# Message-passing layer on one core: the dst table in float32, picked by half blocks on half of the partitions each

## The chip, the cores and the metric

The kernel runs on one NeuronCore of a Trainium2 chip. The metric is the device time of one execution in microseconds (us). Engines are named as the profile names them: PE (TensorE; PEld are its weight loads), DVE (VectorE), ACT (ScalarE), POOL (GpSimd), SP (SyncE, which here only issues DMAs). "SPq" and "ACTq" are DMA issues of these two queues.

## The reference, cut to what matters

```python
h = relu(layernorm(x))                                   # x: 12500 nodes x 64
e = silu(concat(h[src], h[dst], dist) @ eW1 + eb1)       # 212500 edges, eW1: 129 x 128
e = silu(e @ eW2 + eb2)                                  # 128 -> 128
agg = segment_sum(e, src, 12500)
out = x + silu(concat(h, agg) @ nW1 + nb1) @ nW2 + nb2
```

The edges come sorted by dst. All is float32.

## The kernel before, in words

The first product is taken apart: `h[src] @ eW1[:64]` and `h[dst] @ eW1[64:128]` are computed once for each node and kept in two DRAM tables, `ta` (with the bias `eb1` in it) and `tb`. Each entry is held as three bfloat16 numbers (high, middle and low part of the float32 value), 384 numbers in a row. Node n has the place l = n // 100 in the bucket b = n mod 100, so there are 100 buckets of 125 nodes. The work has four stages.

1. **Prologue** (pools `pro`, `norm`, `nab`, `nps`). x is loaded and normalised in five pieces of 20 buckets. `product(1, ...)` makes `tb` for four buckets at a time: matmuls, a copy of the high part (L183), then the rest and the two lower parts (L187 to L190), then a DMA (L192). From src and dst it makes the rows that the blocks compare with (`rows`), for each block the lowest dst of its window (`base_i`), and from the edge weights their three bfloat16 parts (`aux`, `parts3` on DVE and ACT).
2. **Sends.** The edges go in 208 blocks of 1024. `load(s + 2, 1)` issues on SP, for block s, the compare rows three blocks ahead (`bc`, L378) and the window of 112 rows of `tb` and the weight rows of `pick` two blocks ahead (`win` L384, `pick` L386). The start of the window is a register value that SP loads from `base_i` (L383). `count(s + 1)` makes on DVE the one-hot matrix `pick` of dst within the window (L395), the one-hot matrix of the src bucket (`oh`, L397), its running count (`run`, L400) and the count at each edge's own bucket (L408). `send(s)` reads the rank of each edge (L427), multiplies `pick` by `win` (`qp`, L435: for 128 edges three matmuls, one for each bfloat16 part, over 112 node rows and three rows more, which hold the edge weights' parts in `pick` and the weight's row of eW1 in `win`), copies the result to `qs` (ACT, L442), sets the target rows `to` (DVE, L445) and scatters each 128 edges with one indirect DMA from POOL to the DRAM table `q` of the chunk (L454), in which each bucket has a piece of its own. `to` has 4 buffers and `qs` 8, so four blocks of either.
3. **Steps.** The blocks form 11 chunks: the first of 8 blocks, with one tile of 128 rows for each bucket, the others of 20 blocks, with two tiles. When all of a chunk's rows are in DRAM they are read back in 25 batches of four buckets (`fetch`: `qt` from `q`, L499, and `a3` from `ta`, L504, both on SP, five batches ahead). A step takes four tiles of 128 edges: the place within the bucket is spread over the partitions and made one-hot (`s_lr` L521, `s_one_t` L526), the row of `ta` is added while the tile is transposed (`s_pt` L535, L542), then silu, eW2, silu (`s_p2` L573), and the segment sum by one more one-hot matrix (`s_one` L553, `s_seg` L587, `s_add` L598).
4. **Nodes.** With the last chunk's batches the node network runs (`nodes`, L325 to L353).

The order on PE, DVE, ACT and SP is the program's own (`manual_schedule`): `turn` lists the parts of a step with four places between them, at which pieces of the sends of the next chunk are put in, spread evenly (`marks`), three pieces for a block. `sources` (the `ta` table) is fed in at the same places, during the first two chunks. In the prologue a scheduler orders the engines.

PSUM: pool `mm` (4 buffers) serves `lr`, `pt`, `qp`, `ab`, `z` and `o` in turn, `p2` has two, `misc` and `seg` one each.

Of the kernel before, what the change touches and what calls it, by code (L numbers as in the profile page):

```python
# [28 lines left out]
F32 = mybir.dt.float32  # L29
F16 = mybir.dt.float16  # L30
BF16 = mybir.dt.bfloat16
I32 = mybir.dt.int32
# [6 lines left out]
P = 128  # L39
L = 125  # L40
WL = 112
BLK = 1024
TB = BLK // P
# [14 lines left out]
def tile_gnn(ctx: ExitStack, tc: tile.TileContext, x, src, dst, ew, eW1, eb1, eW2, eb2, nW1, nb1, nW2, nb2, out):  # L58
# [39 lines left out]
    def rows16(dma, to, of):  # L98

        for part in (slice(0, WL), slice(WL, L)):  # L100
            dma(to[part], of[part])
# [10 lines left out]
    eb1r = const.tile([1, 2, H], F32, name="eb1r")  # L112
    for t in range(2):
        nc.gpsimd.dma_start(eb1r[:, t, :], rows_of(eb1, 1))
# [31 lines left out]
    nc.vector.tensor_copy(nodes1, nodes_i)  # L146
    ones = const.tile([1, P], F32, name="ones")
# [15 lines left out]
    tb = dram.tile([P * NB, 3 * H], BF16, name="tb")  # L163
    rows = dram.tile([NP, 2, 2, BLK], BF16, name="rows")
    aux = dram.tile([NP, 2, 3, BLK], BF16, name="aux")
# [3 lines left out]
    def product(s, b0, hr, ps, tag, sb, sb2, queue):  # L169

        parts = sb2.tile([P, G, 3, H], BF16, name="parts")
        by = parts.rearrange("l (i a) s h -> l a i s h", a=2)
        rest = sb.tile([P, 2, G // 2, H], F32, name="prest", tag="e1")
        abs_ = []
        for a in range(2):

            half = slice(a * D, (a + 1) * D)
            ab = ps.tile([P, G // 2, H], F32, name="ab", tag=tag)
            if s == 0:
                nc.tensor.matmul(ab, ones, eb1r, start=True, stop=False)  # L180
            for i in range(G // 2):
                nc.tensor.matmul(ab[:, i], hr[half, i, :], w1[half, s, :], start=s == 1, stop=s == 1 or i == G // 2 - 1)
            nc.scalar.copy(by[:, a, :, 0, :], ab)  # L183
            abs_.append(ab)
        yield
        for a in range(2):
            nc.vector.tensor_tensor(rest[:, a], abs_[a], by[:, a, :, 0, :], op=OP.subtract)  # L187
# [9 lines left out]
    base_i = const.tile([1, 2, NP], I32, name="base_i")  # L197
    NW = 4
    wins = [const.tile([P, 3, H], BF16, name=f"win{i}") for i in range(NW)]

    with tc.tile_pool(name="pro", bufs=1) as pro, tc.tile_pool(name="norm", bufs=2) as np_, tc.tile_pool(
# [12 lines left out]
        ewR = pro.tile([NP, PAIR], F32, name="ewR")  # L214
        pad_i = pro.tile([1, PAD], I32, name="pad_i")
        nc.gpsimd.memset(pad_i, N)
        pad_f = pro.tile([1, PAD], F32, name="pad_f", tag="pad_i")
        nc.gpsimd.memset(pad_f, 0.0)
        vec = lambda v, lo, n, m: bass.AP(tensor=v.tensor, offset=v.offset + lo, ap=[[m, n], [1, m]])
        for to, v, pad in (  # L220
            (dstR, dst, vec(dst, E - PAD, 1, PAD)),
            (srcR, src, pad_i),
            (ewR, ew, pad_f),
# [41 lines left out]
        fv = f.rearrange("p (g e) -> p g e", g=2)  # L265
        lo = pro.tile([NP, 2], F32, name="lo")
        nc.vector.tensor_reduce(lo, fv, AX.X, OP.min)
        nc.vector.tensor_scalar(lo, lo, float(N - WL), None, op0=OP.min)
        hi = pro.tile([NP, 2], F32, name="hi")
        nc.vector.tensor_reduce(hi, fv, AX.X, OP.max)  # L270
        lot = nps.tile([1, 2, NP], F32, name="lot", tag="tr")
        for g in range(2):
# [5 lines left out]
        nc.vector.tensor_tensor(  # L278
            rowsS[:, :, 0, :], fv, lo[:, :, None].to_broadcast([NP, 2, BLK]), op=OP.subtract
        )  # L280
# [15 lines left out]
        auxS = pro.tile([NP, 2, 3, BLK], BF16, name="auxS")  # L296
        ev = ewR.rearrange("p (g e) -> p g e", g=2)
        parts3(pro, auxS[:, :, 0, :], auxS[:, :, 1, :], auxS[:, :, 2, :], ev, [NP, 2, BLK], tag="t")
        nc.sync.dma_start(aux, auxS)


# [12 lines left out]


        d3 = pro.tile([P, 3, H], BF16, name="d3")
        parts3(pro, d3[:, 0, :], d3[:, 1, :], d3[:, 2, :], w1d, [P, H])
        for win in wins:
            nc.sync.dma_start(win[WL : WL + 3, :, :], d3[:3, :, :])

# [36 lines left out]
    with tc.tile_pool(name="ld", bufs=4) as ld, tc.tile_pool(name="ld2", bufs=NQ) as ld2, tc.tile_pool(  # L357
# [14 lines left out]
        def load(s, ahead=0):  # L372

            if s + ahead < nblocks:
                p, g = (s + ahead) // 2, (s + ahead) % 2
                bc = ld.tile([P, 2, BLK], BF16, name="bc")
                r = rows[p, g]
                nc.sync.dma_start(bc[:WL], bass.AP(tensor=r.tensor, offset=r.offset, ap=[[0, WL], [1, 2 * BLK]]))  # L378
                blk[s + ahead] = [bc]
            if 0 <= s < nblocks:  # L380
                p, g = s // 2, s % 2
                win = wins[s % NW]
                at = nc.sync.value_load(base_i[:, g, p : p + 1], min_val=0, max_val=N - WL)  # L383
                nc.sync.dma_start(win[:WL].rearrange("p s f -> p (s f)"), tb[bass.ds(at, WL), :])  # L384
                pick = ld.tile([P, BLK], BF16, name="pick")
                nc.sync.dma_start(pick[WL : WL + 3, :], aux[p, g])  # L386
                blk[s] += [win, pick]

        def count(s):
# [4 lines left out]
            bc, win, pick = blk[s]  # L394
            nc.vector.tensor_scalar(pick[:WL, :], bc[:WL, 0, :], part[:WL, :], None, op0=OP.is_equal)  # L395
            oh = wk.tile([NB, BLK], F16, name="oh")
            nc.vector.tensor_scalar(oh, bc[:NB, 1, :], part[:NB, :], None, op0=OP.is_equal)  # L397
            yield
            run = wk.tile([NB, BLK], F16, name="run")
# [17 lines left out]
        def send(s):  # L417
# [4 lines left out]
            _, win, pick, run = blk.pop(s)  # L422
# [5 lines left out]
            yield  # L428
            for t0 in range(0, nt, G):
                qs = qsp.tile([P, G, W], F32, name="qs")  # L430
                qp = mm.tile([P, G, H], F32, name="qp", tag="mm")
                m = min(G, nt - t0)
                for t in range(m):
                    for i in range(3):
                        nc.tensor.matmul(  # L435
                            qp[:, t, :],
                            pick[: WL + 3, (t0 + t) * P : (t0 + t + 1) * P],
                            win[: WL + 3, i, :],
                            start=i == 0,
                            stop=i == 2,  # L440
                        )
                nc.scalar.copy(qs[:, :m, :H], qp[:, :m, :])  # L442
# [380 lines left out]
```

## Time and profile before

| | |
|---|---|
| median of 3 runs | 3321.53 us (3317.69 to 3334.8) |
| the profiled execution | 2708.9 us, its span 2706.9 us |
| mean granted TensorE clock in the profile | 0.915 |
| busy: PE, PEld, DVE, ACT, POOL | 2321.1, 2168.2, 1846.2, 1204.1, 1723.0 us |
| indirect DMAs of POOL (L454) | 1661 of 1030 ns |
| `qp` matmuls (L435) | 4983 of 227 ns |
| DMA | 612.85 MB, mean 226 GB/s |

The duration of a matmul is that of one passing through a pipeline, so matmuls that follow each other overlap: what one costs is read from where the next group starts in the timeline. The profiled execution is shorter than the runs by 612.6 us; all durations and places in time below are the profiled one's.

### The profile page before, as it was taken

Reading aid. Unit: us, or ns where it says so; the run is one execution under the profiler, and the core shown is the slowest. Engines: PE = TensorE matmul, PEld = TensorE weight load, DVE = VectorE, ACT = ScalarE, POOL = GpSimd, SP = SyncE. Lnnn points to the kernel's source line nnn. Section 1 sums busy time; section 2 is a strip of 40 time slices with the busy share of each in tenths; the row PEclk is TensorE's granted clock in tenths of the full one; section 3 lists DMA queues with packets and bytes.
Section 4 is the critical chain, followed back from the end, with each engine's and each line's share of the span. In section 5 each row is a group of like instructions: output and inputs, shape, how many; then the busy total and the mean of one; then the engine's idle time right before and its main releaser. Section 6 shows DMA issues by size and latency. Waiting matters only on the chain. (4 is left out here: it accounts for less than half of the span.)

```text
span 2706.9 us, 61144 instructions
## 1 busy us (share of the span) xinstructions
PE 2321.1 (86%) x23583; PEld 2168.2 (80%) x23583; DVE 1846.2 (68%) x3287; ACT 1204.1 (44%) x2247; POOL 1723.0 (64%) x1691
## 2 busy tenths in 40 slices
PE   1656688799799699799979979979979979979998
PEld 0445577799699699799879979979979979978886
DVE  5745468688588588678768768868858868743332
ACT  2522234355355355355445435535535545534442
POOL 1036577777777777777777777777777777750000
PEclk9755689899899899999989989989989989989998
DMA  6477867987787697697797787788688758644441
GB/s 180 170 210 208 246 226 227 284 276 231 237 280 244 211 288 247 200 312 245 214 293 254 224 274 252 246 247 269 229 248 272 244 185 267 216 173 127 137 128 33
DMA packets 388692, 612.85 MB, mean 226 GB/s; under 512 B 47232, under 2 KB 294401, under 8 KB 387877
## 3 DMA queue, kind: packets, MB, share of 16 engines
q1 hardware_dynamic: 269560, 423.47, 48.7%
q0 software_dynamic: 53760, 122.94, 13.3%
q10 hardware_dynamic: 65074, 62.46, 9.4%
q8 instruction: 188, 3.08, 0.5%
q14 instruction: 110, 0.90, 0.1%
HBM read 393.49 MB, written 215.18 MB: 225 GB/s over the span
## 5 line engine op out<-in xcount | busy, mean ns | idle before, releaser
L454 POOL DMA_INDIRECT q<-qs,to x1661 | 1710.3, 1030 | 679.2 <-issue 386.4
L546 ACT ACTIVATE e<-pt 128x512 f32<-128x512 f32 x525 | 313.7, 597 | 926.5 <-PE pt L542 765.1
L573 PE MATMUL p<-w,e 128*128 128x128 f32 x4200 | 578.7, 282 | 102.3 <-ACT p L567 102.3
L573 PEld LDWEIGHTS p<-w,e 128*128 128x128 f32 x4200 | 523.6, 196 | 117.1 <-ACT p L567 104.3
L526 DVE TENSOR_SCALAR oneT<-lr,part 125x512 bf16<-125x512 f32 x525 | 392.3, 747 | 325.8 <-PE lr L521 325.7
L587 PE MATMUL seg<-one,e 128*128 128x125 f32 x4200 | 581.2, 282 | 19.8 <-DVE aggT L598 14.6
L587 PEld LDWEIGHTS seg<-one,e 128*128 128x128 f32 x4200 | 523.6, 196 | 22.6 <-ACT qs L442 11.7
L400 DVE TENSOR_TENSOR_SCAN run<-oh,end,misc 100x1024 f16<-100x1024 f16 x197 | 461.1, 2340 | 6.4 <-PE misc L427 5.8
L542 PE MATMUL pt<-oneT,a 125*128 125x256 bf16 (+1 forms) x3300 | 440.1, 272 | 0.0
L435 PE MATMUL qp<-win,pick 115*128 115x128 bf16 x4983 | 369.1, 227 | 37.1 <-DVE oneT L526 30.4
L442 ACT COPY qs<-qp 128x512 f32<-128x512 f32 x416 | 243.3, 585 | 286.5 <-PE qp L435 218.3
L435 PEld LDWEIGHTS <-pick 115*128 115x128 bf16 x4983 | 330.4, 102 | 45.3 <-issue 40.8
L553 DVE TENSOR_TENSOR one<-nodes,qt 128x500 f32<-128x500 f32 x525 | 352.2, 671 | 0.7 <-PE seg L587 0.5
L542 PEld LDWEIGHTS <-a 125*128 125x128 bf16 x3300 | 317.8, 99 | 33.5
L535 PE MATMUL pt<-ident,qt 128*128 128x128 f32 x2100 | 329.5, 281 | 3.1 <-DVE prest L187 2.2
L577 ACT ACTIVATE e<-p 128x512 f32<-128x512 f32 x525 | 313.2, 597 | 12.9 <-PE p L573 9.6
L567 ACT COPY p<-b2f 128x512 f32<-128x512 f32 x525 | 311.8, 594 | 0.0
L598 DVE TENSOR_TENSOR aggT<-aggT,seg 128x500 f32<-128x500 f32 x250 | 168.2, 673 | 152.5 <-PE seg L587 152.3
L521 PE MATMUL lr<-identb,qt 128*125 128x128 bf16 x2100 | 210.6, 224 | 62.2 <-DMA qt<-q 62.2
L521 PEld LDWEIGHTS <-qt 128*125 128x125 bf16 x2100 | 187.2, 140 | 64.0 <-DMA qt<-q 63.3
L535 PEld LDWEIGHTS pt<-ident,qt 128*128 128x128 f32 x2100 | 227.6, 144 | 4.0 <-DVE prest L187 2.3
L408 DVE TENSOR_TENSOR run<-run,oh 100x1024 f16<-100x1024 f16 x208 | 144.3, 694 | 7.1
(118 smaller groups left out, 1264.4 us busy)
## 6 DMA issues: line engine op xcount, KB each, us to landing
qt<-q SPq DMA_DIRECT2D x250, 576.0 KB
a<-ta SPq DMA_DIRECT2D x275, 384.0 KB
bc<-rows SPq DMA_DIRECT2D x208, 448.0 KB
q<-zeros ACTq DMA_DIRECT2D x40, 1462.5 KB
q<-qs,to POOLq DMA_INDIRECT x1661
win<-tb SPq DMA_DIRECT2D x208, 84.0 KB
tb<-parts SPq DMA_DIRECT2D x25, 384.0 KB
ta<-parts SPq DMA_DIRECT2D x25, 384.0 KB
```

The lines of the kernel that those rows point to most:

```text
L400: nc.vector.tensor_tensor_scan(run, oh, nil.to_broadcast([NB, BLK]), carry.get(c, 0.0), op0=OP.add, op1=OP.add)
L435: nc.tensor.matmul(qp[:, t, :], pick[: WL + 3, (t0 + t) * P : (t0 + t + 1) * P], win[: WL + 3, i, :], start=i == 0, stop=i == 2,)
L454: i = nc.gpsimd.indirect_dma_start(out=q[:], out_offset=bass.IndirectOffsetOnAxis(ap=to[:k, t : t + 1], axis=0), in_=qs[:k, t - t0, :], in ...
L521: nc.tensor.matmul(lr[:L, t, :], loc[:, at : at + 1].to_broadcast([P, L]), identb, start=True, stop=True)
L526: nc.vector.tensor_scalar(oneT, st[k].pop("lr")[:L], part1[:L, :], None, op0=OP.is_equal)
L535: nc.tensor.matmul(pt[:, t, :], qt[:, j, :H], ident, is_transpose=True, start=t == 0, stop=False, skip_group_check=True)
L542: nc.tensor.matmul(pt[:, cols, :], a3[:L, b, i, :], oneT[:, cols, :], start=False, stop=i == 2, skip_group_check=True)
L546: nc.scalar.activation(e1, pt, AF.Silu)
L553: nc.vector.tensor_tensor(one, nodes1[:, None, :].to_broadcast([P, G, L]), qt[:, j : j + G, H : H + 1].to_broadcast([P, G, L]), op=OP.is_e ...
L573: nc.tensor.matmul(p2[:, t, :], e1[:, t, :], w2, start=False, stop=t == G - 1, skip_group_check=True)
L577: nc.scalar.activation(e2, p2, AF.Silu)
L587: nc.tensor.matmul(item[2][:, b, :], e2[:, t, :], one[:, t, :], start=j % n == 0, stop=j % n == n - 1)
```

## The change

`tb` holds plain float32 rows of 128 (512 bytes where there were 768). `product(1, ...)` therefore only copies its PSUM tiles and sends them off. The window of a block is taken apart in two: each half of a block (512 edges) has a window of 48 nodes (`WL`) of its own, the first on partitions 0 to 49, the second on 64 to 113 (`HB = 64`). `pick` is float32 of 128 x 512: one instruction on DVE makes both halves (`same` is the partition's number within its half, `plus` is 1 on a row of ones). Behind the 48 rows stand the edge weight's row, now loaded in float32 straight from the input, and the row of ones, against which `win` holds the weight's row of eW1 and the bias `eb1`. So the bias leaves `product(0, ...)`, and `aux` and its three parts are gone. A tile of 128 edges takes one float32 matmul over 50 rows where there were three bfloat16 ones over 115; the matmuls of the two halves alternate, and all eight of a block stand in one piece of the program (the `qs` copies too), where there were four tiles in each of two pieces.

On SP a block has two DMAs for `bc`, one for `bb` (the bucket rows), two for `win`, each with a register load before it, and two for the weights, where there were three DMAs and one register load. The weights' DMAs (`weights`) follow the DVE instruction that writes `pick`, since they overwrite a row of it.

```diff
-WL = 112
+WL = 48
+HB = 64
+HALF = BLK // 2
...
+    nc.vector.tensor_scalar(plus, part, HB - 0.5, None, op0=OP.is_gt)
+    nc.vector.scalar_tensor_tensor(same, plus, -float(HB), part, op0=OP.mult, op1=OP.add)
+    nc.vector.tensor_scalar(plus, same, float(WL + 1), None, op0=OP.is_equal)
+    nc.vector.scalar_tensor_tensor(same, plus, -1e6, same, op0=OP.mult, op1=OP.add)
...
-    tb = dram.tile([P * NB, 3 * H], BF16, name="tb")
+    tb = dram.tile([P * NB, H], F32, name="tb")
-    aux = dram.tile([NP, 2, 3, BLK], BF16, name="aux")
...
     def product(s, b0, hr, ps, tag, sb, sb2, queue):
...
-            if s == 0:
-                nc.tensor.matmul(ab, ones, eb1r, start=True, stop=False)
...
+        if s:
+            got = sb2.tile([P, G, H], F32, name="got")
+            for a in range(2):
+                nc.scalar.copy(got.rearrange("l (i a) h -> l a i h", a=2)[:, a], abs_[a])
+            yield
+            queue.dma_start(tables[s][:, b0 : b0 + G, :], got)
+            return
...
-    wins = [const.tile([P, 3, H], BF16, name=f"win{i}") for i in range(NW)]
+    wins = [const.tile([P, H], F32, name=f"win{i}") for i in range(NW)]
+    for win in wins:
+        nc.vector.memset(win, 0.0)
+        for a in range(2):
+            for i, row in enumerate((w1d, eb1b)):
+                at = a * HB + WL + i
+                nc.gpsimd.dma_start(win[at : at + 1, :], row[:1, :])
...
-        auxS = pro.tile([NP, 2, 3, BLK], BF16, name="auxS")
-        ev = ewR.rearrange("p (g e) -> p g e", g=2)
-        parts3(pro, auxS[:, :, 0, :], auxS[:, :, 1, :], auxS[:, :, 2, :], ev, [NP, 2, BLK], tag="t")
-        nc.sync.dma_start(aux, auxS)
...
         def load(s, ahead=0):
...
-                bc = ld.tile([P, 2, BLK], BF16, name="bc")
-                nc.sync.dma_start(bc[:WL], bass.AP(tensor=r.tensor, offset=r.offset, ap=[[0, WL], [1, 2 * BLK]]))
+                bc = ld.tile([P, HALF], BF16, name="bc")
+                for a in range(2):
+                    of = bass.AP(tensor=r.tensor, offset=r.offset + a * HALF, ap=[[0, HB], [1, HALF]])
+                    nc.sync.dma_start(bc[a * HB : (a + 1) * HB, :], of)
+                bb = ld.tile([P, BLK], BF16, name="bb")
+                nc.sync.dma_start(bb[:112], bass.AP(tensor=r.tensor, offset=r.offset + BLK, ap=[[0, 112], [1, BLK]]))
...
-                at = nc.sync.value_load(base_i[:, g, p : p + 1], min_val=0, max_val=N - WL)
-                nc.sync.dma_start(win[:WL].rearrange("p s f -> p (s f)"), tb[bass.ds(at, WL), :])
-                pick = ld.tile([P, BLK], BF16, name="pick")
-                nc.sync.dma_start(pick[WL : WL + 3, :], aux[p, g])
+                for a in range(2):
+                    h = 2 * g + a
+                    at = nc.sync.value_load(base_i[:, h, p : p + 1], min_val=0, max_val=N - WL)
+                    nc.sync.dma_start(win[a * HB : a * HB + WL, :], tb[bass.ds(at, WL), :])
+                pick = ld.tile([P, HALF], F32, name="pick")
+        def weights(s):
+            if s < nblocks:
+                pick = blk[s][3]
+                for a in range(2):
+                    e0 = s * BLK + a * HALF
+                    m = min(HALF, E - e0)
+                    if m > 0:
+                        of = bass.AP(tensor=ew.tensor, offset=ew.offset + e0, ap=[[m, 1], [1, m]])
+                        nc.sync.dma_start(pick[a * HB + WL : a * HB + WL + 1, :m], of)
         def count(s):
...
-            nc.vector.tensor_scalar(pick[:WL, :], bc[:WL, 0, :], part[:WL, :], None, op0=OP.is_equal)
+            nc.vector.tensor_scalar(pick, bc, same, plus, op0=OP.is_equal, op1=OP.add)
...
             yield
+            weights(s)
             run = wk.tile([NB, BLK], F16, name="run")
...
         def send(s):
...
+            qps = [mm.tile([P, G, H], F32, name="qp", tag="mm") for _ in range(2)]
+            for t in range(G):
+                for a in range(2):
+                    half = slice(a * HB, a * HB + WL + 2)
+                    if a * G + t < nt:
+                        nc.tensor.matmul(
+                            qps[a][:, t, :], pick[half, t * P : (t + 1) * P], win[half, :], start=True, stop=True
+                        )
+            halves = []
             for t0 in range(0, nt, G):
-                for t in range(m):
-                    for i in range(3):
-                        nc.tensor.matmul(
-                            qp[:, t, :],
-                            pick[: WL + 3, (t0 + t) * P : (t0 + t + 1) * P],
-                            win[: WL + 3, i, :],
-                            start=i == 0,
-                            stop=i == 2,
-                        )
-                nc.scalar.copy(qs[:, :m, :H], qp[:, :m, :])
+                nc.scalar.copy(qs[:, :m, :H], qps[t0 // G][:, :m, :])
```

## The prediction

> **What bounds the kernel now.** I read the page first: its span, the busy times and the costliest group.
>
> ```profile
> span 2706.9 us, 61144 instructions
> ...
> PE 2321.1 (86%) x23583; PEld 2168.2 (80%) x23583; DVE 1846.2 (68%) x3287; ACT 1204.1 (44%) x2247; POOL 1723.0 (64%) x1691
> ...
> L454 POOL DMA_INDIRECT q<-qs,to x1661 | 1710.3, 1030 | 679.2 <-issue 386.4
> ```
>
> PE looks like the bound. But a POOL that is busy 64% of the span may be full while it has work, so I asked what POOL waited for (total us, times, longest us):
>
> ```profile
> POOL q L454 <- issue: 386.4, 1267, 0.4
> POOL q L454 <- ACT qs L442: 154.8, 18, 143.2
> POOL q L454 <- DMA q<-qs,to: 36.5, 110, 1.7
> ```
>
> The 143.2 us is the time ahead of the first scatter. The rest is almost all a fixed 0.30 us ahead of each one. The timeline of POOL gives the ends and the rhythm:
>
> ```profile
> 172.13 1.17 POOL L454 DMA_INDIRECT q<-qs,to  x1 [143.24 <-ACT qs L442]
> ...
> 1356.63 0.97 POOL L454 DMA_INDIRECT q<-qs,to  x1 [0.30 <-issue]
> 1357.91 0.96 POOL L454 DMA_INDIRECT q<-qs,to  x1 [0.30 <-issue]
> ...
> 2417.58 0.88 POOL L454 DMA_INDIRECT q<-qs,to  x1 [0.30 <-issue]
> ```
>
> 1661 x (1.030 + 0.305) = 2217 us, and with the few longer gaps (32 us, nearly all before 350 us) that is the whole way from 172.1 to 2418.5. **POOL's scatters are the bound for 83% of the span**; ahead of them lies a prologue of 172 us, after them 288 us of the last chunk's steps on PE. A chunk of 160 scatters takes 213.9 us (a long PE gap ends at 726.3, 940.4, 1154.2, 1368.2). PE has slack: between 500 and 2000 us the table of windows gives it 1355.9 us busy of 1500, so 20.6 us idle for each chunk. That idle time is POOL's doing. SP stands at the chunk's first fetch until the last scatter has landed:
>
> ```profile
> 1322.87 0.34 SPq L386 DMA_DIRECT2D pick<-aux  x1
> 1359.07 0.39 SPq L499 DMA_DIRECT2D qt<-q  x1
> ```
>
> **What the skill says.** "SBUF — State Buffer" (Who interferes with whom): POOL builds the descriptors of its DMAs itself, and DVE instructions in a two-port mode lock it out. The trace agrees: scatters that met the one-hot instruction L397 lasted 1.17 us on average, those that met no DVE instruction 0.97. "VectorE: DVE Perf Modes" (The perf-mode tier table): `tensor_scalar` runs at four elements a cycle for bfloat16, two for float32. By this `pick` (512 float32 in place of 1024 bfloat16) keeps its 256 cycles and its 0.483 us, and holds POOL as before; no run shows the float32 form. "TensorE: Matmul & The Clock Gate" (Part 3): matmuls on different row groups run concurrently. "TensorEngine Tiling (Array Packing)" (Key Properties): a change of the tiling mode drains the array. For both the trace has a number:
>
> ```profile
> 141.70 1.55 PE L182 MATMUL ab<-w,hT 64*128 64x128 f32 x8 [0.86 <-DVE prest L187]
> ...
> 166.31 1.22 PE L182 MATMUL ab<-w,hr 64*128 64x128 f32 x4 [6.80 <-DMA hr<-hd]
> ...
> 1502.06 1.06 PE L573 MATMUL p<-w,e 128*128 128x128 f32 x8
> 1502.95 0.83 PE L435 MATMUL qp<-win,pick 115*128 115x128 bf16 x12
> 1503.62 1.11 PE L587 MATMUL seg<-one,e 128*128 128x125 f32 x8
> ```
>
> At the same clock (0.5) eight passes on both halves of the partitions take 1.55 us where four on one half take 1.22: halves do run beside each other. Starts in the last three lines: 12 bfloat16 matmuls cost 0.67 us, four float32 ones (two passes each) 0.89. In the tail, matmuls of 128 and 64 rows alternate (L341 at 2600.46, L342 at 2601.08, L573 at 2601.69): 0.62 us for two passes of 250 columns, which at 0.111 us for 128 are worth 0.43, so 0.19 us for a change of mode.
>
> **The change, part by part.**
> *Prologue.* From 40 to 100 us DVE is busy 57.8 of 60 us; then, to 148.35 us, the groups of `tb` go at 3.0 us each (13 DMAs in 38.9 us on SP), a round of ACT, DVE, ACT, DVE, DMA with two buffers. Gone are 25 x (2 x 0.42 + 0.69) = 38 us of DVE (L187, L190), 25 x 0.62 = 16 us of ACT (L188), two DVE and two ACT instructions of 2.3 and 1.9 us for `aux`, and 3.3 + 1.25 + 0.83 MB of DMA. What is left for a group is 3 x 0.375 = 1.1 us of ACT and a DMA of two thirds of the bytes: estimate 1.8 us a group, 45 us for 25, from the first at 57 us to about 104, plus 3 us for 16 new POOL DMAs (some 0.5 us each, as L127) that stand ahead of `pad_i` and so of ACT's first copy: the last `tb` DMA at 107 instead of 148. I take **-41 us** (-55 to -20). Late next: the zero fills that fill the DMA engines just then (0.92 to 0.98 busy at 150 to 160 and 180 to 220 us).
> *First chunk's sends (to 350 us).* 50 bias matmuls at 1.21 us for two passes leave PE. But SP issues seven DMAs a block for three, at 0.34 to 0.42 us, and a second register load (0.97 us between bc and win): 4.6 us for 2.1 to 2.5. SP's issues here already wait for landings (L386 for the zero fills 76.1 us). POOL had 30 us of gaps here. I take **+8 us** (-15 to +40).
> *Matmuls.* A block's 24 cost 1.34 us. Eight float32 ones cost 0.89 + 2 x 0.19 = 1.27 us if the halves overlap fully, 1.78 + 0.38 = 2.16 if not at all. For 20 blocks -1 to +16 us, against 20.6 us of idle PE: **0** on the path; with less cover the upper end would be on it in full.
> *ACT, PSUM.* Two copies of 0.586 us now come together, and `qp` takes two of `mm`'s four buffers at once: half a block less of run-ahead, hidden by POOL's queue of up to four blocks. DVE: if `pick` ran at one element a cycle, 0.27 us x 20 more on an engine busy 75%: 0. POOL's 1661 scatters stay at 1.335 us.
> *The new wait.* The weights' DMAs wait on DVE's `pick`, one block (9.4 us of PE's work) ahead of their use; behind them on SP are the next fetch and loads. In mid-chunk that hides a landing. At a chunk's start it does not: in program order the weights of the new chunk's second block stand behind the fetch at which SP stands still. So POOL has only the first block in hand, 8 x 1.335 = 10.7 us from about 1.5 us before SP moves. After that: fetch and a3 0.9 us, weights 0.7, landing behind 960 KB (PE resumed at 1368.2, 9.2 us after SP: my bound; I take 5), matmuls 1.3, copy 0.6: first rows at 8.5, bound 12.7, against 9.2. **+1 us** x 10 chunks (0 to 4 each) = +10.
> *Tail.* No `qp` in it: 0.
> Sum: 2708.9 - 41 + 8 + 10 = 2685.9 us. The median of the runs is 612.6 us above the profiled execution, and nothing in the profile says why; I carry the -23 us over as it is: **3298 us**.
>
> **Rivals.**
> 1. *Slower: the weights behind the fetch.* If they land later than about 6 us after SP moves, POOL idles by the rest at each chunk. From 5 us each it outweighs the gain by the 0.5% bound. At 10 us: 3321.5 - 33 + 100 = 3389. For it: one descriptor row behind two large transfers, SP in order. Against: the weights stand directly behind the first fetch.
> 2. *PE becomes the bound*, if the halves don't overlap and the longer runs are a slower PE: (2.16 - 1.34) x 208 = 171 us, 3459. Against: the 1.55 us line.
> 3. *No change*: the prologue's gain is eaten by the zero fills and SP's longer list: 3321.
> 4. *The longer runs are bound by DMA*, busy 0.8 here: bc, win, tb, aux are 33 MB of 613, 5.4%, at most -179 us; half of it: 3230.
> 5. *The fallback* (`general_sums`), if 512 edges span over 48 nodes: 17 edges a node make 30. Under 1%, and milliseconds.
>
> **How the numbers follow.** Forecast 0.53 (own range 3262 to 3330), rival 1 0.17, 2 0.06, 3 0.12, 4 0.12. Half a per cent, 16.6 us, is about what a measurement of this kernel tells from no change. Faster: 0.7 of the forecast and rival 4, 0.49. Same: 0.27 of the forecast and most of rival 3, 0.25. Slower: 0.26. The range 3205 to 3385 leaves out rival 2 and about half of 1 and 4.
>
> **What would show it.** First scatter near 131 us, scatters at 1.33 us with gaps only before 350 us and up to 4 us at the ten chunk starts, `qp` blocks of 1.3 us, 288 us after the last scatter. Wrong would be: POOL gaps in mid-chunk, a first scatter after 155, a chunk other than 214 us.

## The result, and the profile after

| | before | after |
|---|---|---|
| median of the timed runs | 3326.3 us (3317.69 to 3334.8, 4 runs) | 3425.45 us (3413.78 to 3436.86, 4 runs) |
| ratio, 95% interval | | 1.0299 (1.026 to 1.0338): slower |
| profiled execution, span | 2708.9 us, 2706.9 us | 3436.86 us, 3435.0 us |

The forecast was 3298 us, in a range from 3205 to 3385: wrong, and on the wrong side. The table also holds the reason. The profiled execution of after is like its timed runs. That of before, from which every step was worked out, took 18% less than the runs it was to stand for. The experiments met two kinds of chip: on three of them PE paused again and again and the kernel before took 3320 us or more, on two it did not and the same kernel took 2710. (The recorded expectations call a chip with pauses "gated".) Each chip was met once, for one set of runs, so that this belongs to the chip, and not to the hour, is the likely reading and not shown. The trace of before is like those from chips without pauses; its timed runs, and all of after's here, are like those from chips with them. Ratios below are between runs on one and the same chip; traces that are set side by side are in part from different chips of one kind.

The page of after, in the lines that answer to those shown of before (span, busy times, granted TensorE clock in tenths, costliest groups):

```profile
span 3435.0 us, 60065 instructions
...
PE 2690.6 (78%) x21824; PEld 2372.3 (69%) x21824; DVE 1837.9 (54%) x3217; ACT 1169.7 (34%) x2218; POOL 1736.2 (51%) x1705
...
PEclk9556768887998889899888888888888888889999
...
L481 POOL DMA_INDIRECT q<-qs,to x1661 | 1716.8, 1034 | 1379.0 <-issue 610.6
...
L600 PE MATMUL p<-w,e 128*128 128x128 f32 x4200 | 681.5, 310 | 51.5 <-issue 46.9
...
L460 PE MATMUL qp<-win,pick 50*128 50x128 f32 x3322 | 396.7, 328 | 257.8 <-issue 203.8
```

A scatter lasts what it did (1034 ns for 1030), but POOL is idle for 1379 us instead of 679. What POOL waited for (total us, times, longest us):

```profile
POOL q L481 <- issue: 610.6, 1438, 8.4
POOL q L481 <- ACT qs L467: 303.3, 91, 8.7
POOL q L481 <- ACT e L604: 141.1, 25, 6.2
```

Before, the only long wait for ACT was the prologue. Now POOL waits some 90 times for the copy of `qp`. Where the "issue" line was a fixed 0.30 us each time, its longest is now 8.4 us. The timeline of POOL:

```profile
146.83 1.24 POOL L481 DMA_INDIRECT q<-qs,to  x1 [112.75 <-DVE pick L419]
...
1528.75 1.47 POOL L481 DMA_INDIRECT q<-qs,to  x1 [5.08 <-issue]
...
1541.49 0.97 POOL L481 DMA_INDIRECT q<-qs,to  x1 [2.12 <-ACT qs L467]
...
1555.53 1.46 POOL L481 DMA_INDIRECT q<-qs,to  x1 [3.59 <-ACT p L594]
...
3129.04 0.89 POOL L481 DMA_INDIRECT q<-qs,to  x1 [0.30 <-issue]
```

Each block has eight scatters, and here a gap of 2 to 5 us stands ahead of each block, in mid-chunk: what the prediction had named as the sign that it is wrong. In all there are 199 gaps of over 1.5 us, for 208 blocks; in the trace of before there were 6. From first to last scatter it is 2983 us instead of 2246.

### The profile page after: what moved, and what is told of

Its sections match the earlier page's. It is cut to its first block, busy times and chain, and to the rows that moved or that the text cites. A ratio compares the mean times of both kernels' runs of the same rounds, so it can differ in the third digit from the quotient of the medians.

```text
span 3435.0 us, 60065 instructions
## 1 busy us (share of the span) xinstructions
PE 2690.6 (78%) x21824; PEld 2372.3 (69%) x21824; DVE 1837.9 (54%) x3217; ACT 1169.7 (34%) x2218; POOL 1736.2 (51%) x1705
## 5 line engine op out<-in xcount | busy, mean ns | idle before, releaser
L481 POOL DMA_INDIRECT q<-qs,to x1661 | 1716.8, 1034 | 1379.0 <-issue 610.6
L600 PE MATMUL p<-w,e 128*128 128x128 f32 x4200 | 681.5, 310 | 51.5 <-issue 46.9
L614 PE MATMUL seg<-one,e 128*128 128x125 f32 x4200 | 664.1, 305 | 58.1 <-issue 44.2
L600 PEld LDWEIGHTS p<-w,e 128*128 128x128 f32 x4200 | 609.9, 221 | 96.6 <-issue 76.8
L614 PEld LDWEIGHTS seg<-one,e 128*128 128x128 f32 x4200 | 602.1, 219 | 71.3 <-issue 60.5
L460 PE MATMUL qp<-win,pick 50*128 50x128 f32 x3322 | 396.7, 328 | 257.8 <-issue 203.8
L569 PE MATMUL pt<-oneT,a 125*128 125x256 bf16 (+1 forms) x3300 | 514.9, 294 | 79.2 <-issue 77.4
L460 PEld LDWEIGHTS qp<-win,pick 50*128 50x128 f32 x3322 | 300.0, 217 | 339.3 <-issue 299.5
L562 PE MATMUL pt<-ident,qt 128*128 128x128 f32 x2100 | 379.9, 307 | 56.1 <-issue 28.9
L562 PEld LDWEIGHTS pt<-ident,qt 128*128 128x128 f32 x2100 | 260.8, 160 | 68.3 <-issue 36.0
L548 PE MATMUL lr<-identb,qt 128*125 128x128 bf16 x2100 | 246.9, 243 | 53.7 <-issue 32.3
```

Source lines behind the costliest of these rows:

```text
L460: nc.tensor.matmul(qps[a][:, t, :], pick[half, t * P : (t + 1) * P], win[half, :], start=True, stop=True)
L481: i = nc.gpsimd.indirect_dma_start(out=q[:], out_offset=bass.IndirectOffsetOnAxis(ap=to[:k, t : t + 1], axis=0), in_=qs[:k, t - t0, :], in ...
L548: nc.tensor.matmul(lr[:L, t, :], loc[:, at : at + 1].to_broadcast([P, L]), identb, start=True, stop=True)
L562: nc.tensor.matmul(pt[:, t, :], qt[:, j, :H], ident, is_transpose=True, start=t == 0, stop=False, skip_group_check=True)
L569: nc.tensor.matmul(pt[:, cols, :], a3[:L, b, i, :], oneT[:, cols, :], start=False, stop=i == 2, skip_group_check=True)
L600: nc.tensor.matmul(p2[:, t, :], e1[:, t, :], w2, start=False, stop=t == G - 1, skip_group_check=True)
```

## The experiments

### The kernel before, once more

No edit; a second profile of the kernel before, on a chip where the runs of before beside it took 3325.25 us.

> The kernel before, unchanged, profiled a second time. Its profiled execution took 2708.9 us at a mean TensorE clock of 0.915, its timed runs 3318 to 3335 us. Theory A (the kernel before has two regimes, and the timed runs are in the slow one): a profile near 3320 us, with a lower clock, scatters well over 1.335 us apart and PE stalls like those of the kernel after (starts 0.70 us apart, once per block). Theory B (the profile was simply an outlier of a kernel bound by POOL): again scatters at 1.335 us apart, and a time of 3320 us that nothing in the profile explains.

Measured: 3321.08 us, ratio 0.9981 (0.9958 to 1.0004). Theory A holds. Its page:

```profile
span 3309.9 us, 61144 instructions
...
PE 2677.2 (81%) x23583; PEld 2372.9 (72%) x23583; DVE 1858.0 (56%) x3287; ACT 1196.0 (36%) x2247; POOL 1738.1 (53%) x1691
...
PEclk9555778889898989899988988988999989899998
...
L454 POOL DMA_INDIRECT q<-qs,to x1661 | 1725.5, 1039 | 1253.3 <-issue 569.9
```

Same instructions, 603 us longer, and POOL idle for 1253 us. One pause, in the timeline of PE (start, us, the idle time before in brackets):

```profile
713.24 1.06 PE L573 MATMUL p<-w,e 128*128 128x128 f32 x8
714.30 1.23 PE L587 MATMUL seg<-one,e 128*128 128x125 f32 x8
715.37 0.19 PE L427 MATMUL misc<-ones,run 100*128 100x1 f16 x2
715.77 0.24 PE L427 MATMUL misc<-ones,run 100*128 100x1 f16 x4 [0.21 <-issue]
716.49 0.19 PE L427 MATMUL misc<-ones,run 100*128 100x1 f16 x2 [0.48 <-issue]
716.54 0.31 PE L521 MATMUL lr<-identb,qt 128*125 128x128 bf16 x2
717.22 0.32 PE L521 MATMUL lr<-identb,qt 128*125 128x128 bf16 x2 [0.37 <-issue]
717.37 0.39 PE L535 MATMUL pt<-ident,qt 128*128 128x128 f32 x2
718.64 0.58 PE L535 MATMUL pt<-ident,qt 128*128 128x128 f32 x2 [0.88 <-issue]
```

Read the starts: 715.77, 716.49, 717.22: each time a few instructions, then nothing until 0.72 us later, whatever line it is. A record is one instruction of PE in the trace. I count as a pause three or more gaps of over 0.4 us between successive starts of PE's matmul records, with less than 1 us from the end of one gap to the start of the next. Between first and last scatter there are 173 of them, 755 us in all; in after 157, 697 us; in the trace of before that was predicted from, one, of 3 us. From the end of one gap to the end of the next it is mostly about 0.72 us (322 of 607 distances lie between 0.6 and 0.85) or twice that (237). Within pauses the six main steps start 4.3 to 5.0 records a microsecond (weight loads counted), each about the same, where outside they start 15 to 25. So a pause is not a slow pass: PE starts instructions of any kind at a low rate. The granted clock also falls to half, for 772 us of the main part, where it was 359 in the trace that was predicted from.

With that, the main part (first to last scatter) on such a chip can be taken apart by PE's records: the sum of the gaps of over 0.4 us between starts, whether in a pause or not, and what is left, the running time, for `qp` and for all other steps. "Half clock" is the time in the main part at half the granted clock; it lies across the other columns.

| chip with pauses, us | before the first scatter | main part | gaps over 0.4 | `qp` running | other steps running | half clock | tail |
|---|---|---|---|---|---|---|---|
| before (again) | 171.7 | 2836.4 | 766 | 322 | 1749 | 772 | 301.8 |
| after | 146.8 | 2983.1 | 864 | 281 | 1839 | 1038 | 305.1 |

The prologue gains 25 us and `qp` 41. The other steps, which the change does not touch, take 90 us more, and the gaps 98 more. The clock is at half for 266 us longer, which fits the 90, but is not shown to be all of it. The gaps also move: those that follow a `qp` record come to 411 us in after for 199 before, all others to 452 for 567. The windows of the two traces, first to last scatter (us, then busy us of PE, PEld, DVE, ACT and POOL, PE clock, DMA share, GB/s), before and after:

```profile
171.70:3008.10 2836.40, 2319.81 (x21067) 2083.81 (x21065) 1649.91 (x2949) 1011.14 (x1890) 1725.51 (x1661) 0.86 0.61 193
```

```profile
146.80:3129.90 2983.10, 2344.15 (x19288) 2088.54 (x19287) 1664.23 (x2944) 1002.24 (x1886) 1716.79 (x1661) 0.83 0.57 174
```

PE is busy longer with fewer matmuls, at a clock of 0.83 for 0.86, and the transfers use less of the DMA engines: not them.

### Three edits of after on a chip with pauses

All beside before at 3325.25 us.

```diff
             for t in range(G):
-                for a in range(2):
...
+            for a in range(2):
+                for t in range(G):
```

> After, but the eight passes of the first half of the block come first and then the eight of the second, instead of in turns between the two halves of the partitions, so no two neighbouring passes lie on different halves. Theory 1 (stalls come from the two halves of PE working at once): the stalls go and the time falls towards the kernel before, under 3340 us. Theory 2 (stalls are set off by the loads or are in the kernel before too): the stalls stay, and the time rises by up to the lost overlap, 1.07 us per block or 0 to 220 us: 3430 to 3640 us.

Measured: 3436.65 us, 1.0341 (1.0311 to 1.0372), in the range of theory 2. Against the trace of after, `qp` runs 100 us longer without the overlap, the gaps shrink by 88, the clock is at half for 996 us. The pauses don't come from two halves at work at once, and the lost overlap hardly shows.

```diff
-                pick = ld.tile([P, HALF], F32, name="pick")
-                blk[s] += [win, pick]
+                blk[s] += [win, picks[s % NW]]
+                weights(s)
...
-            nc.vector.tensor_scalar(pick, bc, same, plus, op0=OP.is_equal, op1=OP.add)
+            for a in range(2):
+                rows_a = slice(a * HB, a * HB + WL)
+                nc.vector.tensor_scalar(pick[rows_a, :], bc[rows_a, :], same[rows_a, :], None, op0=OP.is_equal)
```

> After, but the weights' rows are loaded with the windows, two blocks ahead, into four pick tiles that keep their row of ones; DVE writes only the 48 rows of each half, in two instructions of 48 partitions for one of 128. The weights' DMA then waits for no DVE instruction, and no pass for a late weights' DMA. Theory 1 (weights behind the fetch at each chunk start, 6 to 7.7 us each, 10 times): 3350 to 3370 us. Theory 2 (the stalls of PE once per block are the cost, and the weights are one of several loads): unchanged within 20 us, 3405 to 3445 us. Theory 3 (PE stalls are set off by the weights' one-row DMAs coming in the middle of a block's work): under 3330 us.

Measured: 3423.02 us, 1.0283 (1.0254 to 1.0311). Theory 2: the weights' wait is not what costs here.

```diff
-                for a in range(2):
-                    of = bass.AP(tensor=r.tensor, offset=r.offset + a * HALF, ap=[[0, HB], [1, HALF]])
-                    nc.sync.dma_start(bc[a * HB : (a + 1) * HB, :], of)
+                nc.sync.dma_start(bc, bass.AP(tensor=r.tensor, offset=r.offset, ap=[[HALF, 2], [0, HB], [1, HALF]]))
...
+                    of = bass.AP(tensor=ew.tensor, offset=ew.offset + s * BLK, ap=[[HALF, 2], [1, HALF]])
+                    nc.sync.dma_start(pick[WL : HB + WL + 1 : HB, :], of)
```

> After, but the two broadcasts of the local destinations are one DMA, and the two rows of weights are one DMA: 5 DMAs per block in place of 7, same bytes. Theory 1 (number of DMAs issued by SP is the cost): faster by 2/4 of the added cost, 3370 to 3385 us. Theory 2 (bytes or the arrival of data, not their number): the same, 3415 to 3440 us.

Measured: 3427.93 us, 1.0301 (1.0276 to 1.0327). Two of the four added transfers are gone and nothing is gained: it is not their number.

### The parts of the change, one at a time

These runs were on a chip without pauses (before 2708.31 us): no pause begins in their traces after the first 300 us. The first kernel has `tb` (the expectations call it B) in float32 and no halves, the second the halves and no float32, the third is after with before's pieces.

```diff
-WL = 48
+WL = 112
...
+                    nc.tensor.matmul(
+                        qp[:, t, :], pick[: WL + 2, (t0 + t) * P : (t0 + t + 1) * P], win[: WL + 2, :], start=True, stop=True
+                    )
```

> One part of the change alone: B in float32, weights' rows from the input and bias by a row of ones, but windows of 112 nodes as before, so one float32 pass with 114 rows per group of 128 edges, one transfer of both broadcasts per block, one register load, each half of a block in a piece of its own, and the weights loaded two blocks ahead. Theory 1 (what costs is the halves: two banks of PSUM at once, all 16 passes in one piece, more transfers): the time of before, 3300 to 3340 us. Theory 2 (float32 passes cost PE more than three bf16 ones once PE is gated): as slow as after, 3400 to 3450 us or more.

Measured: 2639.88 us, 0.9743 (0.9723 to 0.9763). The two theories are about chips with pauses; neither is tested here.

```diff
             for t in range(G):
+                for i in range(3):
                     for a in range(2):
...
-                            qps[a][:, t, :], pick[half, t * P : (t + 1) * P], win[half, :], start=True, stop=True
+                                win[half, i, :],
+                                start=i == 0,
+                                stop=i == 2,
```

> The other part alone: the two halves in turns with windows of 48 nodes, but B and the weights still as three bf16 parts (24 passes of 51 rows in turns, bias in A, loads two blocks ahead, two for each window and for the weights' rows). Theory 1 (the halves cost): 3400 to 3450 us. Theory 2 (float32 costs, the halves gain by overlap): under 3330 us.

Measured: 2706.27 us, 0.9996 (0.9984 to 1.0008). The same holds of its theories.

```diff
+            for t0 in range(0, nt, G):
+                qp = mm.tile([P, G, H], F32, name="qp", tag="mm")
+                a = t0 // G
+                half = slice(a * HB, a * HB + WL + 2)
+                for t in range(m):
+                    nc.tensor.matmul(qp[:, t, :], pick[half, t * P : (t + 1) * P], win[half, :], start=True, stop=True)
```

> After, but the passes, the copy and the scatters of each half in a piece of their own as before (one bank of PSUM at a time, no turns). Theory 1 (two banks at once and 16 passes in a row make PE wait): below a_no_turns by 30 us or more, 3340 to 3400 us. Theory 2 (the order of pieces is not what costs): as a_no_turns, 3425 to 3450 us.

Measured: 2784.01 us, 1.0282 (1.0262 to 1.0302). Its `qp` runs 469 us against 246 in after on another chip of this kind: the overlap saves 1.07 us of PE a block. PE's gaps are 222 us for 396, so it now seems to be PE, no longer POOL, that sets the pace. a_no_turns had been run on the other kind of chip, so the two theories are not told apart.

On another chip without pauses (before 2709.06 us) after itself was run, and three kernels again.

> The kernel after, unchanged, beside the kernel before on the same chip. On a chip where PE is gated (before near 3325 us): 3415 to 3440 us as measured. On a chip where it is not (before near 2708 us): theory 1 (the change also costs where POOL sets the pace, by the weights' late row and PE's 16 passes in one piece): 2740 to 2790 us, near a_two_pieces; theory 2 (the loss is one of the gated state alone, and the steps of the prediction hold where its profile was taken): 2660 to 2690 us.

> a_early_weights once more. Gated: as measured, 3415 to 3435 us. Not gated: theory 1 (weights behind the fetch hold qp, then POOL, at each chunk's start and now and then in between): faster than after by 40 us or more. Theory 2 (the weights' wait is hidden there): as after within 15 us.

> f32_no_halves once more. Not gated: 2635 to 2645 us as measured. Gated: theory 1 (passes on half of the rows cost, by the clock and by PE's time): at or below before, 3200 to 3320 us. Theory 2 (float32 passes cost in the gated state): 3400 us or more.

> bf16_halves once more. Not gated: 2702 to 2712 us as measured. Gated: theory 1 (halves cost): 3400 to 3450 us. Theory 2 (the halves gain PE time by overlap and PE sets the pace there): PE's own time for qp is 149 us less than before's, so 3150 to 3250 us.

Measured: after 2700.61 us, 0.9969 (0.9958 to 0.998); with early weights 2664.46 us, 0.9838 (0.9817 to 0.986); float32 without halves 2639.8 us, 0.9738 (0.9714 to 0.9761); halves in bfloat16 2706.11 us, 0.9991 (0.9979 to 1.0003). So after is not slower on chips of the kind that the profile came from, though both its theories missed its time (2660 to 2690 and 2740 to 2790). The early weights gain 36 us on after, where theory 1 had asked for 40. The two others repeat what they took on the first such chip. What PE waited for there in after (total us, times, longest us):

```profile
PE qp L460 <- issue: 125.7, 7, 21.6
...
PE qp L460 <- DMA pick<-in_edge_weight_dram: 52.8, 7, 21.5
```

These 14 waits of up to 21.6 us are the weights behind the fetches; with the weights loaded early both lines are gone, and the main part falls from 2268.5 to 2226.0 us.

The two parts were run once more, on a chip with pauses (before 3422.07 us):

> f32_no_halves on another chip. Gated (before near 3325 us): theory 1 (passes on half of the rows cost there, by the clock and by PE's time): at or below before, 3200 to 3320 us. Theory 2 (float32 passes cost in the gated state): 3400 us or more. Not gated: 2635 to 2645 us as measured.

> bf16_halves on another chip. Gated: theory 1 (halves cost there): 3400 to 3450 us. Theory 2 (the halves gain PE time by overlap and PE sets the pace there): 3150 to 3250 us. Not gated: 2702 to 2712 us as measured.

Measured: without halves 3334.95 us, 0.9778 (0.9719 to 0.9838); halves alone 3523.75 us, 1.0318 (1.0248 to 1.0387). The expected times had been set for before near 3325 us, so only the ratios can be held against them: theory 1 in both. **The halves are what costs on a chip with pauses; float32 gains on both kinds.** "The halves" are here all that comes with them: passes on half of the rows, all passes of a block in one piece of the program with two PSUM tiles at once, and more transfers. The number of transfers and the turns had been ruled out above; half rows and the one piece are not told apart on a chip with pauses. Their windows from first to last scatter, in the same order:

```profile
132.00:3008.50 2876.50, 2336.55 (x19310) 2154.13 (x19310) 1700.69 (x2947) 1007.42 (x1889) 1726.36 (x1661) 0.87 0.60 188
```

```profile
180.30:3239.70 3059.40, 2367.43 (x21077) 2061.29 (x21077) 1711.56 (x3155) 1012.02 (x1889) 1731.37 (x1661) 0.83 0.56 172
```

By the records `qp` runs 200 us in the kernel with halves and 439 in the one without, so 239 less. But the gaps are 954 us for 747 (of which 455 for 217 follow a `qp` record), the clock is at half for 1031 us for 733, and the other steps run 1905 us for 1690. Float32 without halves beats before on both kinds of chip. It beats after on the same chip without pauses (2639.8 for 2700.61 us); with pauses the two never met on one chip, but the ratios to before, 0.9778 and 1.0299, say the same. It is the version to keep.

### PE by itself

Ten stretches of nothing but passes, to see what sets the pauses off.

```diff
+    for dma in (False, True):
+        for kind, n in SECTIONS:
+            idle(25)
...
+            passes(kind, n)
```

> The disputed cost by itself: ten stretches of 700 to 1400 matmul passes of 128 columns back to back, each after 25 us of idle PE; the first five with no transfers at all, the last five while 12.7 MB are loaded. Kinds in each five: bf16 with 115 rows; the same on zeros; float32 with 128 rows; float32 with 50 rows in turns on the two halves; float32 with 50 rows on one half. It computes none of the output. Theory G (PE itself is gated after some 7 us of full use, whatever else runs): pauses of 0.71 us period in the stretches without transfers too, from about 7 us after each stretch's start, at different depth for the kinds. Theory L (the pauses come from the loads: late instructions or slow semaphores): no pauses in the first five stretches, pauses in the last five. Theory R (the state is of the whole chip and not there in every execution): no pauses anywhere.

Measured on a chip without pauses, 1662.32 us. The scheduler moved the idle times and transfers ahead of the passes, so it tells nothing of transfers. It did show float32 passes of 50 rows on one half at a clock of 0.50 for 299 us, with PE busy for 298.22. And it showed the passes in turns in two ways, one after the other (us, busy us of PE, PE clock, DMA share, GB/s):

```profile
343.00:458.00 115.00, 115.00 (x564) 0.50 0.00 1
459.00:540.00 81.00, 80.20 (x1423) 1.00 0.01 2
```

At first a record starts every 204 ns, so the halves hardly overlap, and the clock is at half for 115 us; once they overlap, with a record every 57 ns, it is whole. The second such stretch does the same. I wrote the order out and ran it again, on a chip with pauses:

> pe_alone with the order written out, since there the scheduler had moved the transfers and idle times ahead: ten stretches of back-to-back passes of 128 columns, each after 25 us of idle PE, the last five while 12.7 MB are loaded: bf16 of 115 rows, float32 of 128 rows, float32 of 50 rows in turns on the two halves, bf16 of 51 rows in turns, float32 of 50 rows on one half. It computes none of the output. Gated chip: theory G (PE is gated after some 7 us of full use, whatever else runs): pauses of 0.71 us period in the stretches without transfers too, and more of them for the kinds that keep both halves busy. Theory L (the pauses come from the loads): none in the first five. Not gated: 57, 114, 57 (in turns) and 212 ns per record (one half, at half clock), no pauses.

Measured: 1546.17 us. The windows of the five stretches without transfers (us, busy us of PE, PEld, DVE and POOL, PE clock, DMA share, GB/s):

```profile
38.00:118.00 80.00, 80.00 (x1397) 80.00 (x1398) 0.00 (x0) 0.00 (x0) 1.00 0.01 2
152.00:310.00 158.00, 157.92 (x1400) 157.77 (x1400) 0.19 (x3) 0.00 (x0) 0.99 0.00 1
344.00:480.00 136.00, 136.00 (x2390) 136.00 (x2392) 0.00 (x0) 0.00 (x0) 0.98 0.01 2
515.00:562.00 47.00, 47.00 (x1598) 46.98 (x1594) 0.00 (x0) 0.00 (x0) 0.94 0.02 5
596.00:766.00 170.00, 170.00 (x797) 170.00 (x798) 0.04 (x2) 0.00 (x0) 0.50 0.00 1
```

No pause in 158 us of full PE, on a chip that has them: theory G falls. With 12.7 MB of loads beside it there were four gaps, 8.2 us, in the fastest kind (bfloat16 in turns, a record every 30 ns), and none elsewhere: theory L holds at most for that. The rows also price the passes: a float32 pass is two records, so 226 ns with 128 rows, 114 in turns on halves, 427 on one half. The last line is the other finding: PE full for 170 us, and the clock at half all the time. "TensorE: Matmul & The Clock Gate" of the Trainium skill (Part 1) has the clock at half after 3.4 us without activity, set by how busy PE is; here half of the rows counts as not busy. In turns it does not, as long as the halves overlap: the 115 us of pe_alone, in turns with hardly any overlap, were at half clock too.

In every trace with pauses none begins after the last scatter, though PE then stays full for 300 us. So I took the scatters away, put plain writes in their place, and set scatters beside PE alone, again on a chip with pauses (before 3423.14 us).

```diff
-                    i = nc.gpsimd.indirect_dma_start(
-                        out=q[:],
...
+                    r = (s - chunk_of.index(c)) * BLK + t * P
+                    nc.gpsimd.dma_start(q[r : r + k, :], qs[:k, t - t0, :])
```

(For the first kernel these lines are left out altogether; in both the zeros cover all rows.)

> After without its 1661 scatters (the sums then run over rows of zeros, which are written in full, so the output is not the reference's). Gated chip: theory S (PE's pauses need the scatters: in every gated trace the last pause begins before the last scatter ends, though PE stays full for 300 us more): no pauses of 0.71 us period, and a time of PE's own work, 2350 to 2600 us. Theory G (PE is paused when it is full, whatever runs beside): as many pauses as before, about one per block, 3150 us or more. Not gated: no pauses under either; 2350 to 2600 us, since PE takes POOL's place as the bound.

> After, each scatter replaced by a plain transfer of the same 128 rows of 576 bytes from the same queue into rows in the order of the edges (the order by node is lost, so the output is not the reference's). Gated chip: if the pauses need the scattered form, none are left and the time is near a_no_scatter's; if any writes of that size from POOL's queue bring them, they stay, 3150 us or more. Not gated: no pauses, 2350 to 2700 us.

Measured: without scatters 2795.2 us, 0.8168 (0.8118 to 0.8219); with plain writes 2911.13 us, 0.8507 (0.8455 to 0.856). Neither trace has a pause after 300 us. So the pauses need the scattered form (on this chip; on the two others with pauses the scatters were not taken away). Both times are above what I had expected (2350 to 2600 us, and near the first), since PE now runs into the weights' late rows: `qp` waits 253 us in the first (96.9 named, 156.1 "issue") and 308 in the second.

```diff
+            for _ in range(scatters):
+                d = nc.gpsimd.indirect_dma_start(
+                    out=q[:],
+                    out_offset=bass.IndirectOffsetOnAxis(ap=idx[:, used : used + 1], axis=0),
```

> PE by itself beside scatters: six stretches of back-to-back passes of 128 columns, each after 25 us of idle PE: float32 of 128 rows alone; the same beside 100 scatters of 128 rows; bf16 of 115 rows beside 60; float32 of 50 rows in turns on the halves beside 80; bf16 of 51 rows in turns beside 40; float32 of 128 rows beside 100 scatters and 12.7 MB of loads. It computes none of the output. Gated chip: theory S: pauses in stretches two to six from a few us after the start, none in the first. Theory G: none here either, as in pe_in_order. Not gated: none anywhere.

Measured: 1417.27 us. The windows of float32 passes alone, then of float32 and bfloat16 passes beside scatters (columns as above):

```profile
38.00:195.00 157.00, 157.00 (x1393) 157.00 (x1394) 0.04 (x2) 0.00 (x0) 1.00 0.00 1
230.00:357.00 127.00, 31.83 (x138) 26.48 (x139) 0.00 (x0) 96.10 (x100) 0.54 0.17 58
548.00:623.00 75.00, 15.93 (x120) 10.77 (x118) 0.00 (x0) 57.03 (x60) 0.55 0.17 58
```

Theory S holds: beside back-to-back scatters PE is busy 31.83 us of 127. It starts well and stops after 163, 154, 150 and 141 records (weight loads counted) in the first four stretches with scatters, be that 12.0 or 3.7 us. So it is a number of instructions, more than a time, after which it slows down.

The obvious guess is that PE starves for instructions, whose loading the scatters hold up. They come in packets of 16 KB; alone, one starts at record 159 and then every 256 or so. But the trace does not bear the guess out. Beside the scatters one packet starts in the first 128 us of the float32 stretch, late, at record 192. It has landed at 251.8 us, and from there to 355 us PE still starts only 0.8 records a microsecond, with a packet in hand. In the kernel before on a chip with pauses, 33 of 175 pauses have the start of a packet in them. What the scatters hold up is open, and so is why other chips don't do it.

## Why the prediction was wrong

**The step that failed** is the last of the sum: "The median of the runs is 612.6 us above the profiled execution, and nothing in the profile says why; I carry the -23 us over as it is". The profile could not say it, because its execution had no pauses. The 612.6 us are PE's pauses and its half clock. Between the two spans of before there are 603 us, of which 590 lie in the main part: 460 more of gaps (766 for 306) and 130 more of running (2071 for 1940). They lie on the path: outside the pauses, PE's gaps come to 122 us of the main part's 2836, so it is PE, paused or at work, that sets the pace there, and POOL is idle for 1253 us. So "POOL's scatters are the bound for 83% of the span" does not hold there, and each edit that was costed at 0 for PE's slack had lost its cover.

**Matmuls, "0".** The size was right: running time of `qp` per block is 246.4 / 208 = 1.18 us where PE doesn't pause (forecast 1.27), and 469.3 / 208 = 2.26 without turns (2.16). The cover was not. On the chips with pauses two effects come with the halves that the step didn't have: the clock at half for 266 us more, with 90 us on the other steps, and 98 us more of gaps. (`pick` in float32, taken as 0.483 us like before, took 0.541.)

**On chips like the one that the trace came from** the sum can be checked: forecast -23, measured 2709.06 to 2700.61, so -8.
- Prologue: -41 forecast (bounds -55 to -20), first scatter at 144.5 instead of 172.1, so -28. Without the halves, on the same chip, it comes at 132.9, -39: the cut was sized well, and what comes with the halves takes 11 us back; which of it, is open.
- First chunk, +8, and new wait, +10: the main part grew by 22 (2246.3 to 2268.5). But the weights' wait alone is 42.5, four times its term, for waits of up to 21.6 us where the working took 5 for the landing, and 14 times in ten chunks. It was rival 1. The rest of the main part shrank by 20, which no step had: that the 22 stand so near the 18 of the two terms is luck.
- Tail, 0: 288.4 to 287.7.

**Rivals.** Rival 1's mechanism is real without pauses and costs nothing that can be seen with them. Rival 2 ("PE becomes the bound, if the halves don't overlap and the longer runs are a slower PE", 3459) had the second half right, the longer runs are a slower PE, and wanted the first as well: the halves overlap, and it still ends at 3425. Rival 4, DMA, falls: before has less of it on the chip where it is slower (0.61 busy in the main part for some 0.8).

**What would have told it.** The profiled execution stood 18% below every timed run. That gap was 26 times the sum of all steps, so the range had no ground to lie around 3298; a PE that is busy 86% in the profile was the nearest thing to look for.

What stays open: why the halves bring the half clock. The 0.50 of one half alone in pe_in_order makes it likely that in a pause, when passes come singly, half rows count as too little work. The traces of the whole kernels speak for it. They log the clock in steps of 3.41 us. Take each step at full clock in the main part, sum the columns that its matmuls stream, and look for the one cut-off that best tells whether the next step is at half. With halves alone in bfloat16 it errs in 46 of 552 steps; with each matmul weighted by its rows, in 15. In after it is 28 and 18 of 570, in float32 without halves, whose main steps all have 100 rows or more, 29 and 29 of 628. So rows seem to count, though no experiment changed them alone on a chip with pauses. The rival, that PE simply stands idle more with the block in one piece, is not excluded: it would bring gaps, and the gaps did grow.

## What to carry to other kernels

Compare the profiled execution with the timed runs before reading the profile: where they differ by more than the change is worth, the bound in the trace may not be the bound in the runs. A resource's idle time covers an edit only in the state in which it was seen. Splitting a contraction over the halves of the partitions saves running time on PE, but look at what the granted clock and the gaps do with it: here float32 passes over 114 rows did better than overlapped ones over 50, on both kinds of chip.

## What the runs showed of the hardware that I had not expected

- On some chips PE all but stops beside indirect scatters: on the one where this was taken apart it is 157.00 us busy of 157 alone and 31.83 of 127 beside them, and in the whole kernel it goes in steps of about 0.72 us. With plain writes from the same queue there were no pauses after 300 us, and on two other chips there were none with the scatters either.
- PE full for 170 us with passes of 50 rows on one half gets half the clock (427 ns a float32 pass). In turns on both halves it gets nearly all of it (0.98, 114 ns) where the halves overlap, and half (0.50 for 115 us) where they hardly do.
- Once PE pauses, saved PE time is largely given back: without turns `qp` ran 100 us longer and the kernel took about 11 us more (1.0341 for 1.0299 of before, with intervals that overlap).
